# Masked attention on one core: one 2048-column exponential in place of two of 1024 in three steps of eight

## The chip, the core and the metric

The kernel runs on one core of a Trainium2 chip. The metric is the device time of one execution in microseconds (us). Smaller is better.

## The reference, cut to what matters

Sixteen sequences of 1024 nodes with 128 features pass through three transformer layers with an adjacency mask and then through one graph-attention layer. For one transformer layer:

```
Q, K, V = h @ Wq, h @ Wk, h @ Wv                 # 8 heads of 16
scores  = Q K^T / 4, -inf where adj == 0
attn    = softmax(scores) @ V
x = layer_norm(h + attn @ Wo + bo)
x = layer_norm(x + relu(x @ W1 + b1) @ W2 + b2)
```

The last layer forms its attention from two vectors per node, with the same mask, and is computed by other code. The exponentials that the change touches are those of the softmax in the three transformer layers.

## The kernel before, in words

**Blocks and steps.** One sequence in one transformer layer is a block: 48 blocks (`blocks`, L655), indexed by `m`. A block has 32 steps: two groups `g` of four heads, two halves `qh` of 512 queries, eight tiles `kt` of 128 keys. There are 48 x 32 = 1536 steps. In this text step 26 is the step with number 26 of 0 to 31 in its block; `kt` is that number modulo 8.

**One step** (`score_step`, L415). TensorE (PE) computes the transposed scores of four heads as two pairs, `pp` = 0 and 1. Each pair fills one PSUM buffer `s` of 1024 columns (two matmuls of 512, L423), and there are three such buffers. A pair is masked and exponentiated in one of two ways:

- first pair, `kt` 0, 1, 3, 4 or 6: ScalarE (ACT) takes the exponential straight from PSUM (L430), then GpSimd (POOL) multiplies it by the 0/1 mask (L431);
- second pair, and both pairs for `kt` 2, 5 and 7 (`BOTH_ON_DVE`): VectorE (DVE) adds the mask to the scores from PSUM and writes them to the SBUF tile `e` (L433). ACT then takes the exponential in place (L445).

The tile `e` holds all four heads, 2048 columns side by side; there are six of them. Below, D is a masking addition of DVE (L433), E is an exponential that follows one (L445), and P is an exponential from PSUM (L430). A number is the step; `a` and `b` are the first and second pair.

**When an E is issued.** The additions are put into the list `masked` with a key, and `exponentials` (L441) is called at the end of each step. It issues those whose key is below `2 * step_no - 1`. In the kernel before, the exponential of the first pair of a `BOTH_ON_DVE` step is issued at the end of the same step. The exponential of any second pair is issued at the end of the step after it, behind that step's P.

**Four steps later** (`AHEAD` = 4) PE multiplies `e` with V into the accumulator `acc` (`av_step`, L450). Behind the last such product of a head group and query half, DVE transposes `acc` into `tt` (L461).

**Pieces.** The rest of the work is cut into pieces. At most one of them is issued after a step (`piece`, L691), at step numbers written in `AT` or after a gap. Most pieces put one PE result of 512 columns into the single PSUM buffer `t`, and another engine must empty it before PE can write the next one:

- `transpose_half` (L281): PE transposes, ACT writes `xT` or `x1T` (L289, L291);
- `split` (L376): PE projects Q or K, ACT writes the upper part `hi` (L385), then DVE subtracts to get `lo` (L386) from the same buffer;
- `v` (L389): ACT writes the values (L392);
- `ffn1` (L500): PE multiplies with half of W1 (L297), ACT writes `hT` (L506);
- `out_proj`, `ffn2`: DVE adds the result to `x` (L329) and takes statistics, POOL normalises.

In 16 of the 48 blocks the pieces of the last layer (`last_tasks`) are interleaved too.

**Order.** PE and ACT run in the order in which the program issues. The order of DVE, POOL and SP in the main loop is planned by the framework when the kernel is built. So on ACT the work of a step is: that step's P, if it has one; the E's that are due; then the ACT part of the step's piece.

Of the kernel before, what the change touches and what calls it, by code (L numbers as in the profile page):

```python
# [36 lines left out]
BOTH_ON_DVE = (2, 5, 7)  # L37
# [78 lines left out]
def fast_path(ctx: ExitStack, tc: tile.TileContext, a: dict, out: bass.AP, flag):  # L116
# [13 lines left out]
    def slot(dtype=F32):  # L130

        return psum.tile([P, N], dtype, tag="s", name="s", bufs=3)
# [13 lines left out]
    def e_tile():  # L146
        return work.tile([P, J, 512], F32, tag="e", name="e", bufs=6)
# [267 lines left out]
    def score_step(step):  # L415
        m, g, qh, kt = step
        e = e_tile()
        q0 = qh * 512
        for pp in range(2):
            q, k = state["Wq", g, pp], state["Wk", g, pp]  # L420
            ps = slot()
            for r in range(2):
                nc.tensor.matmul(ps[:, r * 512:(r + 1) * 512], k[64 * r:64 * r + 64, kt * P:(kt + 1) * P],  # L423
                                 q[64 * r:64 * r + 64, q0:q0 + 512], start=True, stop=True)
            ev = e[:, 2 * pp:2 * pp + 2, :]
            psv = ps.rearrange("p (r q) -> p r q", q=512)
            on_pool = pp == 0 and kt not in BOTH_ON_DVE
            m = (mask01 if on_pool else mask_add)[:, kt, q0:q0 + 512][:, None, :].to_broadcast([P, 2, 512])
            if on_pool:
                nc.scalar.activation(ev, psv, AF.Exp, scale=HD ** -0.5)  # L430
                behind["pool"] = nc.gpsimd.tensor_mul(ev, ev, m).ins  # L431
            else:
                behind["dve"] = nc.vector.tensor_add(ev, psv, m).ins  # L433
                masked.append((2 * step_no[0] + pp + (kt not in BOTH_ON_DVE), ev))
        step_no[0] += 1
        exponentials()
        return e

    masked, step_no = [], [0]

    def exponentials(n=None):  # L441

        while masked and (n is not None or masked[0][0] < 2 * step_no[0] - 1):
            _, ev = masked.pop(0)
            nc.scalar.activation(ev, ev, AF.Exp, scale=HD ** -0.5)  # L445
# [317 lines left out]
    with tc.manual_schedule(engines={mybir.EngineType.PE, mybir.EngineType.Activation}):  # L763
        for m, (b, l) in enumerate(blocks):
# [3 lines left out]
            for at, (g, qh, kt) in enumerate((g, qh, kt) for g, qh in order for kt in range(NT)):  # L768
# [24 lines left out]
                if FIRST <= n < FIRST + 4:  # L793

                    with tc.manual_schedule(engines={mybir.EngineType.DVE}):
                        e = score_step(step)
                        neighbours(4 + n - FIRST)
                        masks(4 + n - FIRST, mask_rows(4 + n - FIRST))
                else:
                    e = score_step(step)  # L800
# [251 lines left out]
```

## Time and profile before

| | |
|---|---|
| median of 3 runs | 3982.76 us (3978.65 to 3982.88) |
| profiled execution, its own time | 3983.09 us |
| its span in the profile | 3981.2 us |
| busy: PE | 3758.5 us (94%) |
| busy: DVE | 3408.3 us (86%) |
| busy: ACT | 3392.8 us (85%) |
| busy: POOL | 3331.4 us (84%) |
| E, 1024 columns (L445) | 2112 of 1060 ns |
| P, 1024 columns (L430) | 960 of 1022 ns |
| D, 1024 columns (L433) | 2112 of 1213 ns |

The span runs from the first to the last instruction of the program. Four engines are busy more than four fifths of it, so an average doesn't say which of them a stage waits for. The granted TensorE clock is 0.9 or more of full speed in all slices of the page but the first and the last, which have 0.8.

### The profile page before, as it was taken

What the parts mean: (1) busy time and instruction counts of PE and PEld (TensorE: products, weight loads), DVE (VectorE), ACT (ScalarE), POOL (GpSimd) and SP (SyncE); (2) the same over time, 40 slices, a digit from 0 to 9 for tenths busy, and PEclk for the clock granted to TensorE, in tenths of its full rate; (3) what the DMA queues carried; (4) which work ended last, traced back from release to release, by engine and by line L of the source; (5) the groups of instructions that cost most, each with busy time, mean ns of one, the idle gap of its engine ahead of it and who ended that gap; (6) DMA issues with size and microseconds to landing.
All of it is one profiled execution on the core that took longest, in us unless ns stands there. A gap on an engine that the chain in (4) does not pass through costs nothing.

```text
span 3981.2 us, 107823 instructions
## 1 busy us (share of the span) xinstructions
PE 3758.5 (94%) x44501; PEld 1558.5 (39%) x44501; DVE 3408.3 (86%) x5326; ACT 3392.8 (85%) x3961; POOL 3331.4 (84%) x3010
## 2 busy tenths in 40 slices
PE   7999999999999999999999999999999999999996
PEld 2333333344443333334444333333444433333345
DVE  7888988988888988988888898888888898898874
ACT  7999999977779999997777999999777799999860
POOL 4788888987789888988778888888877898898875
PEclk8999999999999999999999999999999999999998
DMA  6222222112222222222222222221222212222200
GB/s 163 65 65 53 55 65 63 46 48 65 56 58 57 65 65 54 54 65 55 55 55 55 65 53 56 65 64 45 55 55 55 71 46 62 65 51 58 66 8 20
DMA packets 124465, 233.13 MB, mean 59 GB/s; under 512 B 34624, under 2 KB 73792, under 8 KB 123968
## 3 DMA queue, kind: packets, MB, share of 16 engines
q1 hardware_dynamic: 123056, 225.74, 22.5%
q8 instruction: 354, 5.80, 0.6%
q14 instruction: 143, 1.17, 0.1%
q10 hardware_dynamic: 912, 0.42, 0.0%
HBM read 15.54 MB, written 8.39 MB: 6 GB/s over the span
## 4 chain that ended last, share of the span: by engine, by line
PE 61%; DVE 22%; POOL 9%; ACT 4%; issue 3%; SPq 0%; DMA 0%; DVEq 0%; ACTq 0%; POOLq 0%
PE acc L450 23%; PE t L297 19%; PE s L423 16%; DVE e L433 13%; POOL e L431 3%; POOL x L341 2%; PE t L286 2%; DVE lo L386 2%; DVE st L322 2%; ACT e L445 2%; ACT e L430 2%; DVE tt L461 1%; POOL mv L339 1%; PE s L297 1%; POOL x L345 1%
## 5 line engine op out<-in xcount | busy, mean ns | idle before, releaser
L433 DVE TENSOR_TENSOR e<-s,mask_add 128x1024 f32<-128x1024 f32 x2112 | 2493.6, 1213 | 344.6 <-PE s L423 263.7
L445 ACT ACTIVATE e<-e 128x1024 f32<-128x1024 f32 x2112 | 2203.4, 1060 | 206.1 <-DVE e L433 187.9
L431 POOL TENSOR_TENSOR e<-e,mask 128x1024 f32<-128x1024 f32 x960 | 1933.5, 2026 | 419.0 <-ACT e L430 419.0
L450 PE MATMUL acc<-e,v 128*17 128x512 f32 x12288 | 1627.8, 601 | 73.3 <-DVE tt L461 47.8
L423 PE MATMUL s<-Wq,Wk 64*128 64x512 f32 x6144 | 1185.0, 456 | 58.1 <-DVE e L433 41.3
L430 ACT ACTIVATE e<-s 128x1024 f32<-128x1024 f32 x960 | 980.8, 1022 | 227.5 <-PE s L423 226.5
L423 PEld LDWEIGHTS s<-Wq,Wk 64*128 64x128 f32 x6144 | 501.2, 185 | 1027.9 <-DVE e L433 417.1
L450 PEld LDWEIGHTS acc<-e,v 128*17 128x17 f32 x12288 | 208.6, 95 | 582.1 <-issue 452.0
L341 POOL TENSOR_SCALAR x<-x,mv 128x128 f32<-128x128 f32 x896 | 389.1, 447 | 23.5
L345 POOL TENSOR_TENSOR x<-x,ln_g 128x1024 f32<-128x1024 f32 (+1 forms) x97 | 229.5, 2367 | 25.1 <-PE t L286 22.6
L339 POOL TENSOR_TENSOR mv<-mv,half_neg 128x4 f32<-128x4 f32 x224 | 232.4, 1038 | 18.6
L297 PE MATMUL t<-hd,e 128*32 128x129 f32 x7040 | 208.2, 275 | 1.2
L329 DVE TENSOR_TENSOR x<-t,x 128x512 f32<-128x512 f32 x191 | 130.8, 685 | 86.9 <-PE t L297 86.9
L297 PEld LDWEIGHTS t<-hd,e 128*32 128x32 f32 x7040 | 194.6, 110 | 16.0 <-issue 5.0
L322 DVE BATCH_NORM_STATS2 st<-x 128x6 f32<-128x128 f32 x896 | 197.3, 280 | 3.3
L297 PE MATMUL t<-x1T,W 128*32 128x512 f32 x1520 | 198.0, 592 | 0.0
L297 PEld LDWEIGHTS t<-W,hT 128*32 128x32 f32 x6080 | 170.0, 110 | 58.5 <-issue 45.5
L297 PE MATMUL t<-W,hT 128*32 128x128 f32 x6080 | 183.4, 273 | 0.2 <-DVE x L625 0.2
L286 PE MATMUL t<-identf,x 128*128 128x128 f32 x872 | 151.0, 289 | 34.0 <-DVE lo L386 15.4
L286 PEld LDWEIGHTS t<-identf,x 128*128 128x128 f32 x872 | 92.9, 141 | 230.2 <-issue 108.3
L337 POOL TENSOR_SCALAR mv<-mv 128x4 f32<-128x4 f32 x224 | 53.0, 236 | 124.6 <-DVE mv L324 98.8
L610 DVE SCALAR_TENSOR_TENSOR e<-s,mask 128x1024 f32<-128x1024 f32 x128 | 150.3, 1214 | 5.9 <-PE s L607 5.0
(118 smaller groups left out, 2573.9 us busy)
## 6 DMA issues: line engine op xcount, KB each, us to landing
Wk<-hi SPq DMA_DIRECT2D x384, 128.0 KB
Wk<-lo SPq DMA_DIRECT2D x384, 128.0 KB
Wq<-hi SPq DMA_DIRECT2D x384, 128.0 KB
Wq<-lo SPq DMA_DIRECT2D x384, 128.0 KB
x<-in_x_dram SPq DMA_DIRECT2D x16, 512.0 KB
out_dram<-x SPq DMA_DIRECT2D x31, 256.0 KB
ai<-in_adj_dram SPq DMA_DIRECT2D x8, 512.0 KB
g_rows<-parts SPq DMA_DIRECT2D x124, 4.0 KB
```

The source lines that it names most:

```text
L286: nc.tensor.transpose(ps[:, t * P:(t + 1) * P], src[:, 4 * h + t, :], identf)
L297: nc.tensor.matmul(dst[j:j + SLOT, :], lhsT[:, j:j + SLOT], rhs, start=start, stop=stop)
L322: nc.vector.bn_stats(st[:, t, :], z[:, t, :])
L339: nc.gpsimd.tensor_tensor(v, v, half_neg[:, ts], OP.pow)
L341: nc.gpsimd.tensor_scalar(z[:, t, :], z[:, t, :], mv[:, t, 0:1], mv[:, t, 1:2], op0=OP.add, op1=OP.mult)
L345: nc.gpsimd.tensor_mul(z, z, rows(gain, n))
L423: nc.tensor.matmul(ps[:, r * 512:(r + 1) * 512], k[64 * r:64 * r + 64, kt * P:(kt + 1) * P], q[64 * r:64 * r + 64, q0:q0 + 512], start=Tru ...
L430: nc.scalar.activation(ev, psv, AF.Exp, scale=HD ** -0.5)
L431: behind["pool"] = nc.gpsimd.tensor_mul(ev, ev, m).ins
L433: behind["dve"] = nc.vector.tensor_add(ev, psv, m).ins
L445: nc.scalar.activation(ev, ev, AF.Exp, scale=HD ** -0.5)
L450: nc.tensor.matmul(acc[j * SLOT:j * SLOT + HD + 1, :], v_bufs[m % 2][:, kt, 2 * j + g, :], e[:, j, :], start=first, stop=last)
```

## The change

In a `BOTH_ON_DVE` step the two masked pairs are no longer put on the list one by one. When the second has been added, the whole tile `e` is put on it once, with the key that the second pair has in other steps. One exponential of 2048 columns is then issued at the end of the next step, behind that step's P if there is one. All other steps keep their order. The change adds three lines: the exponential of L445 stands in L448 afterwards.

```diff
                 behind["dve"] = nc.vector.tensor_add(ev, psv, m).ins
-                masked.append((2 * step_no[0] + pp + (kt not in BOTH_ON_DVE), ev))
+                if kt not in BOTH_ON_DVE:
+                    masked.append((2 * step_no[0] + 2, ev))
+                elif pp:
+                    masked.append((2 * step_no[0] + 2, e))
         step_no[0] += 1
         exponentials()
```

## The prediction

> **What bounds the kernel now.** I read the page first: busy shares, costliest groups, then the chain that ended last.
>
> ```profile
> PE 3758.5 (94%) x44501; PEld 1558.5 (39%) x44501; DVE 3408.3 (86%) x5326; ACT 3392.8 (85%) x3961; POOL 3331.4 (84%) x3010
> ...
> PE 61%; DVE 22%; POOL 9%; ACT 4%; issue 3%; SPq 0%; DMA 0%; DVEq 0%; ACTq 0%; POOLq 0%
> ...
> L445 ACT ACTIVATE e<-e 128x1024 f32<-128x1024 f32 x2112 | 2203.4, 1060 | 206.1 <-DVE e L433 187.9
> ...
> L430 ACT ACTIVATE e<-s 128x1024 f32<-128x1024 f32 x960 | 980.8, 1022 | 227.5 <-PE s L423 226.5
> ```
>
> TensorE carries the chain (61%); ACT holds 4% of it and is idle for 3981 - 3393 = 588 us. So a saving on ACT doesn't shorten the run by itself. What counts is *when* ACT gives back what PE waits for.
>
> The timeline repeats: of the 48 blocks about 30 take 73.15 us each from first score to first score. I call these plain. The others, mostly those with pieces of the last layer, take 77 to 99 us. I took the plain block from 1440.7 us apart. A step without a piece takes PE 1.65 us (0.66 for scores, 0.98 for the products with V, by the chain) and a 512-column piece 0.86 more. Summed over its 32 steps, PE stands still for about 4.2 us, mostly behind D (L433) and tt (L461). Next to nothing of that is behind ACT, but in two places ACT is only just in time. The first is the FFN stage, steps 25 to 28:
>
> ```profile
> 1500.96 0.78 ACT L291 ACTIVATE x1T<-t,ln_bc,ln_gc 128x512 f32<-128x512 f32 x1
> ...
> 1501.62 2.01 ACT L445 ACTIVATE e<-e 128x1024 f32<-128x1024 f32 x2
> 1501.79 0.13 PEld L297 LDWEIGHTS t<-x1T,W 128*32 128x32 f32 x4 [0.45 <-ACT x1T L291]
> ...
> 1503.52 0.69 ACT L506 ACTIVATE hT<-t,b 128x512 f32<-128x512 f32 x1
> ...
> 1504.09 1.04 ACT L430 ACTIVATE e<-s 128x1024 f32<-128x1024 f32 x1
> ...
> 1504.99 1.08 ACT L445 ACTIVATE e<-e 128x1024 f32<-128x1024 f32 x1
> ...
> 1505.94 0.71 ACT L506 ACTIVATE hT<-t,b 128x512 f32<-128x512 f32 x1
> ...
> 1506.70 0.13 PEld L297 LDWEIGHTS t<-x1T,W 128*32 128x32 f32 x4 [0.36 <-ACT hT L506]
> ```
>
> The weight load at 1501.79 starts when x1T is done (1501.74), the one at 1506.70 when hT is done (1506.65). PE itself loses nothing yet: 2.50 us a step is its own work. The second is step 11 to 12:
>
> ```profile
> 1467.73 1.05 ACT L445 ACTIVATE e<-e 128x1024 f32<-128x1024 f32 x1
> ...
> 1468.68 0.57 ACT L385 CAST hi<-t 128x512 fp32r<-128x512 f32 x1
> ...
> 1469.29 0.69 DVE L386 TENSOR_TENSOR lo<-t,hi 128x512 fp32r<-128x512 f32 x1
> ...
> 1470.03 0.13 PEld L297 LDWEIGHTS t<-Wo,aT 128*32 128x32 f32 x4 [0.44 <-DVE lo L386]
> ```
>
> E10b, then hi, then lo, then PE's next piece: each starts within 0.1 us of the one before it.
>
> **What the skill says.** The Trainium skill, "ScalarE: Activation LUTs", section "What ACT_TABLE_LOAD costs", prices an ACTIVATE with immediate scale and bias at 186 ns + 0.833 ns a column, and says that back-to-back ones overlap by about 93 ns. The trace agrees roughly: 1039 ns priced, 1060 measured, and in unbroken runs one E starts 947 ns after the one before, an overlap of 113. "Perfetto Trace Analysis", section "Identifying the Most-Contended Engine", warns that matmul busy time is a poor measure because matmuls are pipelined. I therefore used PE's start times, not its 94%.
>
> **The change part by part.** *Size.* 3 of 8 steps have both pairs on DVE: 1536 x 3/8 = 576. Removed are 1152 E's of 1060 ns, added 576 of 2048 columns. No such row is in the trace; 1060 + 1024 x 0.833 = 1913 ns (an estimate with the page's rate; its full price gives 1892; the other end is 2120, nothing saved). I take 1913. The next instruction then starts 1913 - 113 = 1.80 us after it, against 2 x 0.947 = 1.89. ACT's queue gets shorter by only 0.09 us a time, 576 x 0.094 = 54 us in all, and all of that beside other work. Costed at nothing; PE's work covers it, and if ACT were the bound it would be the first rival.
>
> *Order.* This is the larger part. Step 2 before: E1b, E2a; step 3: P3, E2b, piece. After: E1b; P3, E2ab, piece. In step 3, 6 and 0 (of eight) P comes earlier by up to one E, in steps 2, 5 and 7 the piece does. But before, E2a filled time in which ACT waited for D2b: in 252 of the 576 steps ACT stood idle until D of the first pair ended and started E within 0.1 us. Now those columns run when D2b is done too, and whatever stands behind E2ab starts 1.80 us after D2b, not 0.95. Behind it are the piece of that step, the next step's P and its piece. No E comes too late for the products with V: in the plain block each E ends at least 3.1 us before them, and moves by 0.85 at most. POOL waits for P; it gets P earlier after steps 2, 5, 7, and in the step after that (4, 1) up to 0.85 later, where its own queue is mostly 1 to 4 us behind P. No DMA, PSUM read or DVE instruction is added or moved by the program.
>
> *FFN stage.* D23b ends at 1497.76 us, so E23ab runs from 1497.79 and P25 starts at 1499.59, not 1499.10. E24b and x1T follow: x1T at 1501.44, 0.48 late. PE's piece 26, which started right behind x1T, is 0.48 late, and all of PE after it. hT26 and P27 now come almost on time (1503.60 and 1504.17), because E26a is gone from before them. Then E26ab starts at 1504.17 + 0.905 (interval P to E) = 1505.08, hT27 at 1506.88, 0.94 late. The load at 1506.70 had 0.1 us to spare before PE would have stood: PE is 0.83 late in all. **+0.83 us** a plain block.
>
> *Step 12.* D10b ends at 1467.57, E10ab runs from 1467.60, hi starts at 1469.40 in place of 1468.68. lo and the Wo piece follow: **+0.72 us**. DVE waits with lo, so D12 behind it is as late, and PE's later stalls behind D don't absorb it.
>
> *Small ones.* Step 19's evacuation of v comes 0.74 late with some 0.67 to spare: +0.07. P4 with its PSUM buffer: +0.1. Gain: scores 25 stood 0.17 us behind P24, which comes 0.6 earlier: -0.17.
>
> Sum for a plain block: 0.83 + 0.72 + 0.17 - 0.17 = 1.55, for 30 of them 47 us. For the other 18 I did the same comparison ACT instruction by instruction: producers held at their times, ACT's queue laid anew with the measured intervals, each delay less the room before its user. It gives 42 us, from hi 11, v 19, x1T, hT and P (the same count gives the plain ones 55, before gains). P's and evacuations that come early end at most 17 us of PE's waiting in the whole run; I take 8. 47 + 42 - 8 = 81 us. I round down to **75** because some delays will meet PE stalls that exist already. On the profiled execution's own 3983.1 us (span 3981.2 and 1.9 around it, 0.3 above the median) this is 4058 us, **slower by 1.9%**.
>
> **Rivals.**
>
> *ACT's saving reaches the end.* If ACT were the bound, 54 us would go: 3929. For it: ACT waits for PE 227 us, it is 85% busy, and in the FFN stage it is busy without a break. Against: its 4% of the chain. A faster kernel would come from P and the evacuations that move ahead: up to 17 us, 3966. It decides from the point where PE waits for P or t in steps 2, 3, 5, 6, 7, 0 for longer than it does behind E2ab's followers. I counted such waits at few places. Chance 0.07.
>
> *Absorbed.* PE has 4.2 us of stalls in a plain block; if the 1.55 fall into them, the time is 3983 to 3995. Against: those stalls wait for DVE, which waits for PE's scores and for lo, so they move along. Chance 0.09, half of it within 0.2%.
>
> *The DVE plan changes.* DVE's order is planned at build time. If lo is placed behind D12b, as hi is late, it loses a D (1.2 us) less what is left of its wait: about 0.5 us x 48 = 24 us more, 4082 or above; a better place for it may give back the 0.72 x 48 = 35, so 4025. Chance 0.24 for either, both slower.
>
> *The change doesn't do what it says.* If the E's key kept E2a's columns in their step, nothing would be late. The key 2s + 2 is popped only in step s + 1, so I give this no chance of its own.
>
> **How the numbers follow.** The case as worked out has 0.60, with a range of its own of 4020 to 4095 (from half of the counted delays to all of them and a 2048-column E 0.1 us longer, which adds 0.1 x 3 places x 48 = 14 us). With the DVE plan it reaches 4110, with part of the absorbed case 4000. About 0.2% (8 us) is what a measurement of this kernel can tell from no change. Faster by more: 0.07; within: 0.05; slower: 0.88.
>
> **What would show it.** Right: 576 rows of 2048 columns near 1.9 us and 960 of 1024 in L448; ACT's busy time down by about 54 us with a longer span; plain blocks of 74.2 to 75 us; longer waits of PE's loads for hT (L506), x1T (L291) and lo (L386); the piece in step 28 and step 12 with PE idle before it. Wrong: plain blocks at 73.2 us or below, or a growth that stands behind D (L433) or POOL alone.

## The result, and the profile after

| | before | after |
|---|---|---|
| median of 4 runs | 3982.82 us (3978.65 to 3987.35) | 4076.66 us (4074.93 to 4079.71) |
| profiled execution | 3983.09 us | 4076.49 us |
| its span | 3981.2 us | 4074.7 us |
| a plain block (one taken from 1440.7 us before, from 1477.0 us after) | 73.15 us | 74.70 us |

The ratio is 1.0236 with a 95% interval of 1.0218 to 1.0254: slower by 93.8 us, or 2.4%. The forecast was 4058 us, with a range of 4000 to 4110.

The page of the kernel after, busy shares and then the chain that ended last:

```profile
PE 3782.8 (93%) x44501; PEld 1540.8 (38%) x44501; DVE 3407.2 (84%) x5326; ACT 3333.4 (82%) x3385; POOL 3341.1 (82%) x3010
...
PE 55%; DVE 22%; ACT 8%; POOL 8%; issue 7%; SPq 0%; DMA 0%; ACTq 0%; DVEq 0%; POOLq 0%
```

ACT was busy for 3392.8 us and is now busy for 3333.4. It does 59.4 us less and the run takes 94 us more. At the same time its share of the chain doubles, from 4% to 8%, and that of PE falls from 61% to 55%. An engine with less work has become the one that others wait for. The groups of ACT with shapes kept apart (busy us, mean ns, idle before and its releasers):

```profile
L448 ACT ACTIVATE e<-e 128x2048 f32<-128x2048 f32 x576 | 1101.4, 1912 | 80.1 <-DVE e L433 65.1 <-POOL mv L339 11.8
L448 ACT ACTIVATE e<-e 128x1024 f32<-128x1024 f32 x960 | 1006.6, 1061 | 24.1 <-DVE e L433 24.1
```

The wide E takes 1912 ns, and in unbroken runs the next instruction starts 1.80 us after it. Both are what was estimated. Of the 104 us that ACT now stands idle ahead of E's, 80 belong to the wide ones, 576 of 1536 rows. In all, E's wait less than before (206 us on the page of before). The waiting has moved to P: ACT stands idle ahead of it for 410 us instead of 227, 352 of them until PE's scores come.

The view of waits shows who pays (waiting engine and line, releaser: us in total, times, longest):

```profile
PEld t L297 <- ACT hT L509: 71.7, 119, 0.9
...
PE t L297 <- DVE lo L386: 45.1, 50, 0.9
...
PEld t L297 <- ACT x1T L291: 38.1, 47, 1.2
```

Before, the same waits were 42.8 us for hT, 3.5 us for lo (the matmul's own) and 19.6 us for x1T, with the same counts for hT and x1T. (The weight loads' own waits for lo fell, from 48.0 to 25.2 us; load and matmul together went from 51.5 to 70.3.) These are the pieces whose input comes from ACT, directly or through `hi`. The sums point to places; they don't price them, since a weight load can wait while PE still has work (see the FFN stage below).

*Where in the block.* A step is counted from the start of its scores to the start of the next step's scores. The table has what each step takes after, minus what it takes before, as the median over the plain blocks:

| step | 12 | 16 | 17 | 20 | 24 | 25 | 26 | 28 | all 32 |
|---|---|---|---|---|---|---|---|---|---|
| us | +1.11 | -0.31 | +0.22 | +0.10 | -0.09 | +0.11 | +0.27 | +0.16 | +1.57 |

The others are within 0.03. There are 47 distances from one block to the next. 29 are plain and add 45.4 us together. The other 18 add 46.7 us, and there the mean is +1.04 at step 12, +0.68 at 25, +0.50 at 28, +0.38 at 29, +0.34 at 26, -0.22 at 27, and -0.51 at 5. What is left of the 93.5 us between the spans lies at the ends of the run.

*Step 12.* The timeline of the kernel after, a plain block whose scores of step 12 start at 1653.86:

```profile
1653.35 1.91 ACT L448 ACTIVATE e<-e 128x2048 f32<-128x2048 f32 x1 [0.41 <-DVE e L433]
...
1655.17 0.57 ACT L385 CAST hi<-t 128x512 fp32r<-128x512 f32 x1
1655.22 1.16 DVE L433 TENSOR_TENSOR e<-s,mask_add 128x1024 f32<-128x1024 f32 x1
...
1656.30 0.68 DVE L386 TENSOR_TENSOR lo<-t,hi 128x512 fp32r<-128x512 f32 x1
...
1657.12 1.08 PE L297 MATMUL t<-Wo,aT 128*32 128x128 f32 x32 [0.91 <-DVE lo L386]
```

E10ab holds ACT until hi can start at 1655.17. That is 1.31 us after the scores; in the same block before it was 0.52 us (1614.96 against 1614.44). But hi is done at 1655.74 and lo starts only at 1656.30. D12b (1655.22) was put ahead of it and runs until 1656.38. Before, DVE did lo, then the reciprocals (L463), then D12b; now it does the reciprocals, D12b, then lo. So the Wo piece comes 3.26 us after the scores instead of 2.16. The same block in the kernel before:

```profile
1615.57 0.69 DVE L386 TENSOR_TENSOR lo<-t,hi 128x512 fp32r<-128x512 f32 x1
...
1616.34 1.17 DVE L433 TENSOR_TENSOR e<-s,mask_add 128x1024 f32<-128x1024 f32 x1
...
1616.60 1.07 PE L297 MATMUL t<-Wo,aT 128*32 128x128 f32 x32
```

*FFN stage.* The kernel after, steps 25 to 28 of another plain block:

```profile
1535.26 1.91 ACT L448 ACTIVATE e<-e 128x2048 f32<-128x2048 f32 x1 [0.18 <-DVE e L433]
...
1538.93 0.77 ACT L291 ACTIVATE x1T<-t,ln_bc,ln_gc 128x512 f32<-128x512 f32 x1
...
1539.76 0.16 PEld L297 LDWEIGHTS t<-x1T,W 128*32 128x32 f32 x8 [0.98 <-ACT x1T L291]
1539.76 1.06 PE L297 MATMUL t<-x1T,W 128*32 128x512 f32 x8
...
1542.38 1.91 ACT L448 ACTIVATE e<-e 128x2048 f32<-128x2048 f32 x1
1544.18 0.69 ACT L509 ACTIVATE hT<-t,b 128x512 f32<-128x512 f32 x1
...
1544.92 1.06 PE L297 MATMUL t<-x1T,W 128*32 128x512 f32 x8
```

x1T ends at 1539.70. The weight load and the first matmul of the piece start together at 1539.76, and the products with V ahead of them had ended 0.06 us before, so PE had run out of work. Behind hT, which stands right behind E26ab and ends at 1544.87, the load and the matmul also start together, just as the products with V end. In the kernel before, the loads started at 1501.79 and 1506.70 (shown in the prediction), and the matmuls later:

```profile
1502.08 1.04 PE L297 MATMUL t<-x1T,W 128*32 128x512 f32 x8
...
1507.08 1.04 PE L297 MATMUL t<-x1T,W 128*32 128x512 f32 x8
```

There the products with V ran on for 0.47 and 0.57 us after the load had started, and the matmul came 0.29 and 0.38 us after its load. That is room which a late x1T or hT uses up before PE loses anything.

### The profile page after: what moved, and what is told of

The parts are those of the page before. It is cut to its first block, busy times and chain, and to the rows that moved or that the text cites. A ratio compares the mean times of both kernels' runs of the same rounds, so it can differ in the third digit from the quotient of the medians.

```text
span 4074.7 us, 107506 instructions
## 1 busy us (share of the span) xinstructions
PE 3782.8 (93%) x44501; PEld 1540.8 (38%) x44501; DVE 3407.2 (84%) x5326; ACT 3333.4 (82%) x3385; POOL 3341.1 (82%) x3010
## 4 chain that ended last, share of the span: by engine, by line
PE 55%; DVE 22%; ACT 8%; POOL 8%; issue 7%; SPq 0%; DMA 0%; ACTq 0%; DVEq 0%; POOLq 0%
PE acc L453 19%; PE t L297 19%; PE s L423 13%; DVE e L433 13%; ACT e L448 3%; ACT e L430 3%; POOL e L431 3%; DVE st L322 2%; POOL x L341 2%; DVE lo L386 2%; DVE tt L464 1%; PE t L286 1%; POOL mv L339 1%; PE s L297 1%; ACT hi L385 1%
## 5 line engine op out<-in xcount | busy, mean ns | idle before, releaser
L448 ACT ACTIVATE e<-e 128x1024 f32<-128x1024 f32 (+1 forms) x1536 | 2103.7, 1380 | 104.2 <-DVE e L433 89.1
```

## Experiments

Every kernel below was run with its own runs of the kernel before, whose medians were 3982.1 to 3982.2 us. "Plain" is the change of a plain block, read as in the table above.

**1. The deferral without the merge.** The change does two things at once: it issues the first pair's E a step later, and it makes one instruction of two. This kernel does only the first.

```diff
-                masked.append((2 * step_no[0] + pp + (kt not in BOTH_ON_DVE), ev))
+                masked.append((2 * step_no[0] + 2, ev))
```

> Both exponentials of a BOTH_ON_DVE step keep their 1024 columns, but both get the key 2s + 2, so the first one also moves to the next step, behind that step's P. Theory A (the time is lost by moving the first exponential behind the point where ACT's next evacuations wait): about as slow as the changed kernel, 4075 to 4090 us, plain blocks 74.7 to 74.9 us, because two exponentials in a row hold ACT for 1.89 us and the one of 2048 for 1.80. Theory B (one long instruction that can't be shared is what costs): back to 3983 to 4000 us, plain blocks 73.2 us.

Measured: 4040.65 us, ratio 1.0149 [1.0132, 1.0166]; plain +1.02 (step 12 +1.11, 16 -0.32, 17 -0.08, 20 0.00, 24 -0.09, 25 +0.11, 26 +0.06, 28 +0.25); the 18 other blocks +25.9. Neither figure came. The deferral is 58 of the 94 us, and the merge, which shortens ACT's work, costs 36 us more. In the plain blocks the timeline tells why. Here the first of DVE's three additions is D23b:

```profile
1516.81 3.46 DVE L433 TENSOR_TENSOR e<-s,mask_add 128x1024 f32<-128x1024 f32 x3
...
1517.80 2.00 ACT L445 ACTIVATE e<-e 128x1024 f32<-128x1024 f32 x2
```

E23a starts at 1517.80 while D23b is still running (to 1518.02). Both E's are done 2.99 us after the start of D23b. In the kernel after, at the same place:

```profile
1533.98 3.45 DVE L433 TENSOR_TENSOR e<-s,mask_add 128x1024 f32<-128x1024 f32 x3
```

E23ab (1535.26, shown above) waits for D23b and ends at 1537.17, 3.19 us after the start of D23b. One instruction waits for the later of its two additions before it does the first column. That is 0.2 us at this place, what steps 26 differ by (0.27 against 0.06). At steps 17 and 20 the join costs 0.30 and 0.10; at step 28 it gives back 0.09. In step 12, hi is only 0.38 us late in this kernel, lo stands behind D12b here too, and the step still loses all of 1.11 us. That pointed to DVE's order.

The plain blocks hold about 15 of the merge's 36 us. The other 21 lie in the 18 other blocks, and the traces show two causes there. In four of them at step 25, and in six at step 28, x1T stands behind a wide E that waits 0.9 us for its second addition, and the step is 0.9 us longer than with the deferral alone: some 9 us. In the same six blocks DVE's order differs. In the kernel before and in the deferral, the last layer's `hd` (L575) stands ahead of D25b and its `parts` (L587) ahead of D29b; in the kernel after, both stand behind. Steps 25 and 29 are 1.24 and 0.82 us longer for it, some 12 us. In one of these blocks, kernel after, step 25:

```profile
1036.87 1.08 PE L297 MATMUL t<-Wo,aT 128*32 128x128 f32 x32 [1.03 <-DVE hd L578]
```

ACT isn't late there: its part of that piece, ahead of `hd`, starts 0.14 to 0.15 us after the scores in all three kernels. No run puts DVE's order back at these two steps, so this split rests on the traces alone.

**2. `lo` ahead of D12b again, with the change.** From the kernel after, DVE is held to the order of the program in these two steps, for all blocks but the first:

```diff
+                    if at == 11 and m:
+                        in_order = tc.manual_schedule(engines={mybir.EngineType.DVE})
+                        in_order.__enter__()
                     e = score_step(step)
...
                 piece()
+                if at == 12 and m:
+                    in_order.__exit__(None, None, None)
```

> The changed kernel, with VectorE held to program order in steps 11 and 12 of each block but the first, so that lo stands ahead of the masking addition of step 12 again, as in the kernel before. Theory A (late hi on ACT, made worse by VectorE's new plan): step 12 still loses what hi's delay of 0.72 us leaves after about 0.28 us of room, 0.44 in place of 1.11, so plain blocks of 74.0 to 74.1 us and about 4045 us. Theory C (the new plan of VectorE is the whole cause at this place): step 12 as long as before, plain blocks near 73.6 us, 4025 us or below.

Measured: 4056.21 us, 1.0183 [1.0166, 1.0200]; plain +0.97, with +0.51 at step 12 and all other steps as after. The timeline, with scores of step 12 at 1644.62:

```profile
1645.93 0.57 ACT L385 CAST hi<-t 128x512 fp32r<-128x512 f32 x1
...
1646.53 0.69 DVE L386 TENSOR_TENSOR lo<-t,hi 128x512 fp32r<-128x512 f32 x1 [0.47 <-ACT hi L385]
...
1647.28 1.08 PE L297 MATMUL t<-Wo,aT 128*32 128x128 f32 x32 [0.30 <-DVE lo L386]
```

hi is as late as after (1.31 us behind the scores), lo follows at once, and the piece comes at 2.66 instead of 3.26. So 0.60 of the 1.11 us is lo's place behind D12b and 0.51 is hi itself. The two don't simply add: behind D12b, lo starts 2.44 us after the scores whether hi is 0.38 us late (experiment 1) or 0.79. The whole kernel gave less than expected, since the 18 other blocks kept their loss in sum (46.8 us, +1.13 at step 12). Five of them lose 0.51 at step 12 now, as the plain ones do. In twelve the loss grew from about 1.1 to 1.5: program order put two transpositions into `aT` (L480) ahead of that of `acc` there. For those twelve this run says nothing on the cause.

**3 to 5. The merge at chosen `kt` only.** Steps of other `kt` keep the two E's and the keys of the kernel before.

```diff
+                if kt in (2,):                 # or (5,), or (5, 7)
+                    if pp:
+                        masked.append((2 * step_no[0] + 2, e))
+                else:
+                    masked.append((2 * step_no[0] + pp + (kt not in BOTH_ON_DVE), ev))
```

> The merge in the steps with kt = 2 alone; kt 5 and 7 as in the kernel before. Theory A (place decides): hi of step 11 and hT of step 27 stand behind these, so steps 12 and 28 stay long, plain blocks 74.4 to 74.8 us, 4045 to 4070 us. Theory B or any cost that goes by the number of merged exponentials: a third of the loss, about 4014 us.

> The merge in the steps with kt = 5 alone; kt 2 and 7 as in the kernel before. Theory A (place decides): nothing that PE waits for stands close behind these four exponentials of a plain block, so plain blocks 73.1 to 73.3 us and 3975 to 3995 us. Any cost that goes by number: a third of the loss, about 4014 us.

> The merge in the steps with kt = 5 and 7; kt 2 as in the kernel before. In the run with kt = 5 alone the loss of a plain block was in step 17, whose second scores wait for P16; P16 stands on ACT behind the late hi of step 14 and the first exponential of step 15 (kt 7). With kt 7 merged too, that exponential no longer stands ahead of P16. Theory A (place decides): step 17 loses 0.2 us in place of 1.17, steps 12 and 28 nothing, steps 24 to 26 about 0.3, so plain blocks 73.3 to 73.5 us and 3990 to 4010 us: faster than kt 5 alone with twice the merges. Any cost that goes by number: two thirds of the loss, about 4045 us.

| merged | median us | ratio | plain, and its steps | other 18 blocks |
|---|---|---|---|---|
| `kt` 2 | 4047.02 | 1.0162 [1.0145, 1.0179] | +1.29: 12 +1.11, 28 +0.16 | +26.2 |
| `kt` 5 | 4018.32 | 1.0087 [1.0071, 1.0104] | +0.87: 16 -0.31, 17 +1.17 | +8.7 |
| `kt` 5, 7 | 4007.24 | 1.0062 [1.0047, 1.0077] | +0.29: 16 -0.31, 17 +0.22, 20 +0.10, 24 -0.10, 25 +0.10, 26 +0.28 | +16.8 |

The cost goes by place, not by number: each of the first two merges a third of the 576 pairs, and one costs 65 us, the other 36. `kt` 2 owns steps 12 and 28 (through E10ab and E26ab). Together with `kt` 5 and 7 it gives the plain 1.57 us again (1.29 + 0.29).

`kt` 5 alone missed its expectation: it costs more than `kt` 5 and 7 together. The timeline of `kt` 5, with scores 17a at 1641.54 and then 17b:

```profile
1642.03 1.01 ACT L430 ACTIVATE e<-s 128x1024 f32<-128x1024 f32 x1
...
1643.10 0.51 PE L423 MATMUL s<-Wq,Wk 64*128 64x512 f32 x2 [1.06 <-ACT e L430]
```

E13ab waits for D13b, so hi14 behind it is 0.85 us late. E14b and E15a follow, and then P16, which runs from 1642.03. Scores 17b can't start before P16 has emptied its PSUM buffer, and PE stands for 1.06 us. When `kt` 7 is merged too, E15a is gone from ahead of P16 and the delay is nearly used up. In the kernel after, that is +0.22. The -0.31 at step 16 is DVE's doing: in these two kernels and in the kernel after, lo 14 stands behind D15b and not ahead of it, so D15b empties its PSUM buffer about 0.34 us before scores 17a start. In the kernel before, 17a wait for it.

**6. The same merge, with the piece first in steps 11 and 25.** From the kernel after, the E's that are due in these two steps are issued behind the step's piece instead of ahead of it, so hi 11 no longer stands behind E10ab, and x1T 25 no longer behind E24b, which has 1024 columns. E23ab is still ahead of x1T 25.

```diff
-        exponentials()
+        if (step_no[0] - 1) % 32 not in (11, 25):
+            exponentials()
...
                 piece()
+                if at in (11, 25):
+                    exponentials()
```

> The changed kernel with all 576 merged exponentials, but in steps 11 and 25 of each block the due exponentials are issued behind the step's piece and not ahead of it, so that hi of step 11 and x1T of step 25 come early on ACT. Theory A: steps 12 and 26 lose nothing, plain blocks 73.2 to 73.5 us, step 12 of the other blocks is repaired too: 4005 to 4030 us. Theory B (the instruction's length, wherever it stands): no repair, 4065 us or above.

Measured: 4012.61 us, 1.0077 [1.0062, 1.0092]; plain +0.19 (step 12 0.00, 26 0.00, 28 +0.18, the others as after); other blocks +22.8. All 576 wide E's are still there, and two changes of order a block take back 64 of the 94 us. In the other blocks too, step 12 is as long as before on average; in six of them step 25 still loses 1.24 us, with `hd` behind D25b. Step 12, with its scores at 1625.96:

```profile
1626.10 0.59 ACT L385 CAST hi<-t 128x512 fp32r<-128x512 f32 x1 [1.05 <-PE t L297]
1626.58 1.92 ACT L449 ACTIVATE e<-e 128x2048 f32<-128x2048 f32 x1
...
1627.04 0.66 DVE L386 TENSOR_TENSOR lo<-t,hi 128x512 fp32r<-128x512 f32 x1
```

hi starts 0.14 us after the scores. lo starts 0.35 us after hi's end, behind a transposition of `acc` on DVE, and the Wo piece comes 2.16 us after the scores, as in the kernel before. DVE's order is that of the kernel before again, with lo ahead of D12b, so this run takes away both parts of the loss at step 12. Whether the same order of pieces would gain something in the kernel before was not run.

**7. The merge in its own step.** The wide E gets the key with which it is issued at the end of its own step, so nothing is deferred and E of the second pair comes a step earlier than before.

```diff
                 elif pp:
-                    masked.append((2 * step_no[0] + 2, e))
+                    masked.append((2 * step_no[0], e))
```

> One exponential of 2048 columns, but issued at the end of its own step, ahead of the next step's P. It needs the second masking addition, so ACT waits for it with the step's piece and the next P behind. Theory A (what counts is what stands behind the late columns on ACT): slower than the changed kernel, since P3, P6 and P0 of every cycle, with 0.3 to 0.6 us of room, come up to 2 us later than before: 4100 to 4250 us. Theory D (moving the first exponential to the next step is what costs, not what it holds up): faster than the changed kernel, 3990 to 4040 us.

Measured: 4371.35 us, 1.0971 [1.0954, 1.0987]; plain +6.84, spread over the block (step 12 +1.54, 15 +1.16, 26 +1.02, 25 +0.87, 20 +0.83, 27 +0.82, 7 +0.62). The direction was right and the size far beyond what I expected. Nothing is gained from not deferring: now ACT stops for D of the second pair, with the step's piece queued behind, and stands idle for 714 us ahead of the wide E's where it was 80. PE waits for both pieces of the FFN stage:

```profile
1813.11 1.07 PE L297 MATMUL t<-x1T,W 128*32 128x512 f32 x8 [0.81 <-ACT x1T L291]
...
1816.44 1.06 PE L297 MATMUL t<-x1T,W 128*32 128x512 f32 x8 [0.61 <-ACT hT L509]
```

So of the two places for a merged E, the change has the better one.

**8 to 10. The gain at step 16, alone.** Both the kernel after and the deferral without the merge gain 0.31 us at step 16. The kernels here have no merge. From the kernel before, the first pair's E is deferred in one or two steps of the block:

```diff
-                masked.append((2 * step_no[0] + pp + (kt not in BOTH_ON_DVE), ev))
+                later = kt not in BOTH_ON_DVE or step_no[0] % 32 in (13, 15)   # or (15,), or (13,)
+                masked.append((2 * step_no[0] + (2 if later else pp), ev))
```

> The kernel before, with two exponentials of 1024 columns kept, and the first of them moved to the next step in steps 13 and 15 of a block alone. In the run with all of them moved, steps 16 and 17 of a plain block were 0.40 us shorter than before, because VectorE's plan sets lo of step 14 behind the addition of step 15, and nothing else in a plain block depends on these two steps. Theory A: plain blocks 72.7 to 72.8 us, about 12 us in all, 3968 to 3975 us, faster than both kernels. Theory that each move costs by itself: slower than before by an eighth to a sixth of that run's loss, 3989 to 3992 us.

> The kernel before, with the first exponential of step 15 of each block moved behind P16, and nothing else. Reading of the run with 13 and 15: P16 is early because this exponential no longer stands ahead of it, so the scores of step 17 find P16's PSUM buffer free and don't wait for the addition of step 15. Then this run has the whole gain: step 16 shorter by 0.3 us, plain blocks 72.7 to 72.8 us, 3965 to 3975 us. If the gain came from VectorE's plan for lo of step 14, as I first read it, this run has none of it: 3978 to 3986 us.

> The kernel before, with the first exponential of step 13 alone moved to the next step, behind P14. Then hi of step 14, the second exponential of step 14, the first of step 15 and P16 all come up to 0.85 us late. If P16 decides: step 17 loses 0.8 to 1.2 us as in the run with the merge at kt = 5, plain blocks 73.8 to 74.1 us, 4005 to 4025 us. If lo of step 14 decides: a gain at step 16 and none of that loss, 3965 to 3980 us.

| deferred | median us | ratio | plain, and its steps |
|---|---|---|---|
| 13 and 15 | 3967.67 | 0.9966 [0.9952, 0.9979] | -0.40: 16 -0.32, 17 -0.07 |
| 15 | 3968.59 | 0.9967 [0.9954, 0.9979] | -0.40: 16 -0.31, 17 -0.08 |
| 13 | 3983.73 | 1.0003 [0.9994, 1.0012] | 0.00 |

The first two are faster than both kernels, by 0.3% against the one before. For the first I had expected the time, but for another reason (a better place of lo 14 on DVE); DVE's order there and in experiment 1 is the same as before, so that reason is wrong for these kernels. The second and third run separate the two steps, and the whole gain is step 15. In the kernel before, around steps 16 and 17:

```profile
1478.80 1.01 ACT L430 ACTIVATE e<-s 128x1024 f32<-128x1024 f32 x1
1479.48 0.89 PE L423 MATMUL s<-Wq,Wk 64*128 64x512 f32 x4 [0.25 <-DVE e L433]
```

E15a (from 1477.86) stands ahead of P16, and scores 17a wait 0.25 us until D15b has emptied a PSUM buffer. With step 15 deferred:

```profile
1618.91 1.02 ACT L430 ACTIVATE e<-s 128x1024 f32<-128x1024 f32 x1
...
1620.22 0.81 PE L423 MATMUL s<-Wq,Wk 64*128 64x512 f32 x4
```

P16 is first. Measured from the block's start it ends at 38.14 us, not 39.10. Scores 17a take the buffer that P16 has emptied and start without a wait, at 1620.22, while D15b still runs (from 1619.26). Their weight load is released by P16.

In the kernel after, the gain at step 16 is not this one. P16 ends at 40.12 us from the block's start there, after 17a have started (39.56); it is D15b that is done by then (39.22), ahead of lo 14 in DVE's new order. Scores 17b then wait for P16, and step 17 gives back 0.22 of the 0.31.

Step 13 missed both figures that I had given. In experiment 4 the merge there cost 0.87 us a plain block; the deferral of E13a, narrow, costs nothing. (Experiment 4 merges three more steps of a block, but only steps 16 and 17 changed there.) E13a is issued behind P14 in both. The timeline of the kernel with step 13 deferred, D13b with the addition behind it and then E13a with the E behind it:

```profile
1474.70 2.32 DVE L433 TENSOR_TENSOR e<-s,mask_add 128x1024 f32<-128x1024 f32 x2
...
1474.98 2.01 ACT L446 ACTIVATE e<-e 128x1024 f32<-128x1024 f32 x2
```

E13a starts 0.28 us after the start of D13b. Measured from the block's start, the narrow one starts at 33.81 us, while D13b runs to 34.73; in experiment 4 the wide one starts at 34.74. So it is the wait for both additions that is dear there, not the later place.

## Why the prediction was right or wrong

The direction and the size held, and so did part of the mechanism: ACT's queue is shorter, but what stands behind a wide E comes later. The other part is that DVE's order changed, for the lo of steps 11 and 14 and for the last layer's pieces; the prediction held that as a rival. The total came this close in part by luck, because errors of both signs cancelled. Point by point:

- **Size of the wide E: right.** 1913 ns and 1.80 us were predicted, 1912 ns and 1.80 us measured. ACT saved 59.4 us where 54 were counted. The page of the Trainium skill, "ScalarE: Activation LUTs", section "What ACT_TABLE_LOAD costs", gives 1892 ns, 20 less than measured; its rate per column agrees (1912 - 1061 = 851 ns for 1024 columns, 0.831 each).
- **Plain block: +1.55 predicted, +1.57 measured, but as a sum of two terms that were off in opposite directions.** The closeness is luck.
- **FFN stage: too dear.** The term was 0.83, less 0.17 gained at scores 25; steps 26 and 28 gave 0.27 and 0.16, and 24 to 28 together 0.45. The step that failed is "PE's piece 26, which started right behind x1T, is 0.48 late". The *load* started right behind x1T. The *matmul* came 0.29 us later, because the products with V ahead of it were still running, and that 0.29 was room. In the kernel after, x1T is 0.53 us later against the scores of its step, near the 0.48 that was predicted, and the matmul 0.24. The same holds for the load at 1506.70, which was given 0.1 us to spare: its matmul came 0.38 us later. hT is 0.52 us later in its step, and the matmul 0.13. The gain at scores 25 came to 0.09 (step 24) and was lost again in step 25 (+0.11).
- **Step 12: too cheap.** The term was 0.72, from hi being late. hi was 0.79 late, but here too the matmul had room in the kernel before: the load at 1616.32, the matmul at 1616.60. That leaves 0.79 - 0.28 = 0.51, and 0.51 is what experiment 2 shows with lo ahead of D12b. The other 0.60 is the rival that the prediction named, "The DVE plan changes": lo went behind D12b. It had priced that at about 0.5 us a block beyond the 0.72, without counting the room, and gave it a total of 4082 us or above, which was not reached.
- **The join was not separated from the deferral.** The prediction saw that E2ab waits for D2b, and charged it as one delay. Experiment 1 gives 58 us for the later place and 36 for the merge. Of the 36, some 24 are the wait for both additions (the timelines show it at steps 17 and 26 of the plain blocks and at steps 25 and 28 of others; at step 20 it is taken from the difference alone), and some 12 are DVE's order in six blocks.
- **Gains: half right.** That P moves ahead and PE gains by it was counted at 8 us for the whole run. Experiments 8 and 9 show that it is real, 0.40 us a plain block, for a buffer that the prediction had not looked at. In the kernel after it didn't come: the 0.31 us at step 16 are from DVE's order.
- **Small terms:** step 20 was 0.07 and came as 0.10; P4 was 0.1 and nothing was seen at step 4.
- **The 18 other blocks:** 42 us predicted, 46.7 measured. Some 12 of these are from DVE's order in six blocks, which was not counted, so the closeness is in part luck here too. Apart from step 12 and the places named in experiment 1, I did not break these down further than by step.
- **The rounding down from 81 to 75** "because some delays will meet PE stalls" went the wrong way. The measured sum is 93.8. Of the 13 us between the two, 5 are the other blocks and 8 the gains taken off for the whole run, which didn't come beyond what the sums over the blocks already hold.

The rival that ACT's saving reaches the end is refuted: the saving was made in full, and every merge that was tried costs time. "Absorbed" fails too. Most of what should be seen in the profile was seen: longer waits for hT, x1T and lo, and in step 12 a PE that is idle for 0.91 us ahead of the piece. For lo it is the matmul that waits longer; the loads' own wait fell. In step 28 the trace shows no idle PE, only a matmul that starts as soon as its load does.

## What to carry to other kernels

Two instructions merged into one save a fixed cost each time (0.09 us here), but the one waits for the later of its two inputs and holds a queue that runs in order for the length of both; look for what stands behind it, and put that first if someone waits for it. Count the room at the *matmul* that uses the result, not at its weight load. When an order is planned by the framework at build time, a delay on one engine can reorder another: compare the order of the neighbours before you explain a loss by the delay alone. The order can change even where nothing is late: six blocks here lost 1.24 us at a step in which ACT's part came on time.

## What the runs showed of the hardware that was not expected

- A weight load that starts within 0.1 us of its producer doesn't mean that TensorE is waiting. Where the matmuls ahead were still running, the matmul came 0.28 to 0.38 us after its load (1616.32 and 1616.60; 1501.79 and 1502.08; 1506.70 and 1507.08). Where they had ended, both started in the same 0.01 us (1539.76).
- The wide E starts 0.09 us after the end of its last addition at four of the five places of a plain block where ACT stands idle for it (E2ab, E10ab, E18ab, E23ab). E13ab starts 0.03 us after it, as the narrow ones do. The trace doesn't settle what makes the difference.
- The overlap of one ACT instruction with the next doesn't grow with its length: 1.91 - 1.80 = 0.11 us behind 2048 columns, and 0.11 us behind 1024.
